# New durations in a planner's list, sums of queries and keys on two engines, and unread products inside the tables

## The chip, the cores and the metric

The kernel runs on one core of one Trainium2 chip. The metric is device microseconds (us) of one launch; one more execution is taken with the hardware profiler, and its trace is what is read here. TensorE (PE) multiplies, with weight loads (PEld) beside it; VectorE (DVE), ScalarE (ACT) and GpSimd (POOL) work elementwise, and SyncE (SP) issues transfers. GpSimd issues the indirect transfers.

## The reference

Two transformer layers on x of 2 x 2048 x 256. Each layer normalises x and adds two things to it: attention and a mixture of experts.

```python
x = L0_attn_x
xn = _layernorm(x, axis=-1)
x = x + _L0_attn_ref(xn, ...) + _L0_ffn_ref(xn, ...)
xn = _layernorm(x, axis=-1)
x = x + _L1_attn_ref(xn, ...) + _L1_ffn_ref(xn, ...)
```

Layer 0 attends causally with 16 heads of 16 over 2048 rows, keys and values shared by groups of four heads; queries and keys come through low-rank matrices and are turned by rotary tables (`x1 * cos - x2 * sin`, `x1 * sin + x2 * cos`). Its experts: each row goes to the best two of eight, with places up to a capacity of 1280 each, `gelu(a) * g`, and a gated sum. Layer 1 attends to 32 fixed patterns with sparsemax, and has eight experts and a shared one. The change touches layer 0 alone.

## The kernel before

**The stages.** Layer 0's attention, and six of its eight experts woven into it, are one hand-made stream (to about 1400 us in the trace); then experts 6 and 7 run; then layer 1, which another planner (class Plan) orders. Layer 1 is not changed.

**What the stream holds.** The attention takes 32 units j (a batch, a block of 512 queries, and a group of heads). For each j: *maxima* (line 530, tile s): TensorE multiplies queries with keys in 64-row halves, VectorE takes each row's maximum from PSUM (line 550); the maxima of a whole j are flipped (mtT) and placed by a transfer into the queries as further rows, so that the scores come out with the maximum subtracted. *Scores* (line 579, tile sc): 128 x 512 products, and ScalarE's exponential (line 589) frees the PSUM bank; there are two such banks. On the diagonal GpSimd masks the result (line 591, affine_select). *Values* (line 594, tile av): four groups of 32 columns side by side. Then VectorE transposes, GpSimd scales (line 616), and the output projection follows (po).

**Preparation.** Groups of 512 rows are fetched, normalised, flipped (tp), and brought to low rank (lw). Cosine and sine *tables* of a block of 512 positions (line 406, tile cs) are spread from 16 partitions to 128: two products with 16 rows, then a copy by ScalarE. A *rotary step* (lines 452 to 475) makes queries or keys: TensorE products (pab), VectorE multiplies with the tables (line 460), GpSimd adds the two halves (line 1016, "the sum"), ScalarE rounds the result (line 467, "the conversion"), GpSimd subtracts to get the remainder (line 474, "the difference"), and SyncE writes both to DRAM, from where the queries and keys are loaded. There are 24 such steps, 8 for keys and 16 for queries.

**Routing and scatters.** When all groups' logits are there, VectorE ranks the experts and computes each row's slot. Then GpSimd scatters 32 tiles of rows to the experts' buffer: for each tile SyncE loads the row (line 729), GpSimd writes a tag (line 733) and issues two indirect transfers (line 736). When all are sent, the woven experts begin: turning (ext), hidden products (exh), down products (exy), scaling, and an indirect accumulation into x1 (line 811).

**What sets the order.** Every instruction is pinned in the order in which the list loop (line 1501) emits it. The loop keeps a modelled clock for each engine (`T`) and picks, among the candidates for TensorE, the one with the least price: its wait, a switch of layout (SWX), and weights such as EXB, IDLE, FILL, RUN. Work of the other engines is emitted by `later` and `flush` (lines 850 and 854) when its inputs are ready in the model. `scatter` (line 1190) emits a tag or a transfer when GpSimd's modelled clock has passed. `add_group` and the due times GRP0 and GRPN say when preparation should come; MOST bounds the lead of maxima, TAIL says how early the woven experts should be done. A score is the unit in which places in the list are given here: "score 192" is after 192 of the 1280 score products.

**Unread products.** Where the model expects TensorE to wait before the woven experts begin, `fill` (line 1476) emits bfloat16 products whose result nobody reads (tile idle), one per 150 modelled ns of wait, unless a share of recent activity is reached; `keep_up` (line 1492) adds them where that share is short. `STREAM` (line 822) says how much each kind of work counts as activity.

Of the kernel before, what the change touches and what calls it, by code (L numbers as in the profile page):

```python
# [11 lines left out]
F32 = mybir.dt.float32  # L12
I32 = mybir.dt.int32
F32R = mybir.dt.float32r
BF16 = mybir.dt.bfloat16
AF = mybir.ActivationFunctionType
ALU = mybir.AluOpType
# [6 lines left out]
P = 128  # L24
# [8 lines left out]
ROW = E + 2  # L33
# [116 lines left out]
def moe_transformer_kernel(  # L150
# [8 lines left out]
    V, A, G, PE, SP = nc.vector, nc.scalar, nc.gpsimd, nc.tensor, nc.sync  # L159
# [23 lines left out]
    ones = keep.tile([P, P], F32, name="ones")  # L183
# [109 lines left out]
    with ExitStack() as actx:  # L293
# [38 lines left out]
        def pin(ins):  # L332
            return tc.keep_in_program_order(ins)

        def mm(*args, **kw):
            pin(PE.matmul(*args, **kw))  # L336
# [62 lines left out]
        def load_tables(blk):  # L399
# [3 lines left out]
            for i, ap in enumerate((cos, sin)):  # L403
                sdma(cs16[blk][0:16, i], ap[0:16, 512 * blk:512 * blk + 512])

        def tables(blk):

            ps = ps2.tile([P, 2, 512], F32, tag="ps2", name="cs128")
            for i in range(2):
                mm(ps[:, i], lhsT=sel16.rearrange("k a b -> k (a b)"), rhs=cs16[blk][0:16, i], start=True, stop=True)  # L410
            pin(A.copy(cs_sb[:, :, 512 * blk:512 * blk + 512], ps))

        def fetch(grp):
# [53 lines left out]
            pin(A.copy(hi, tt[:, 0]))  # L467
            return hi

        def rope_low(tt, r, hi):  # L470
            n = tt.shape[0]
            at = 2048 + 512 * r
            lo = scr[:n, at:at + 512].bitcast(F32R)
            pin(G.tensor_tensor(lo, tt[:, 0], hi.bitcast(F32), ALU.subtract))
            return lo

        kss, qs, vas = {}, {}, {}
# [154 lines left out]
        def add_sum(bq):  # L632
            pin(G.dma_start(x1[0:NT].rearrange("(t p) d -> p t d", p=P)[:, 4 * bq:4 * bq + 4], xos[bq], accum_op=ALU.add))
# [185 lines left out]
        nch = lambda j: 4 * (j // 4 % 4) + 4  # L819
        INF = 10 ** 9  # L820
        HOP, SWITCH, ISSUE, LAND, BYTE = 150, 200, 620, 2300, 0.003
        STREAM = {"v": 0.34, "r64": 0.72, "r128": 0.72, "c": 0.12, "g": 0.2, "f": 0.8, "s": 0.85}
        FULL = dict.fromkeys(("t", "l", "p", "f", "o", "r64", "r128", "v"), "sc")
        T = dict.fromkeys(("PE", "V", "A", "G", "S", "D"), 0)
        model = {"mode": "", "scores": 0.0, "maxima": 0.0, "n": 0}
# [4 lines left out]
        def on(eng, dur, ready=0):  # L830
            T[eng] = max(T[eng], ready) + dur
            return T[eng] + HOP
# [10 lines left out]
        def shift(n, ready):  # L843
            T["D"] = max(T["D"], ready) + n * BYTE
            return T["D"] + LAND - 500
# [4 lines left out]
        def later(eng, dur, ready, f, then=None, rank=1):  # L850
            jobs.append([rank, len(jobs) + model["n"], eng, dur, ready, f, then])
            model["n"] += 1

        def flush():
            now, done = T["PE"], False
            for job in sorted(jobs, key=lambda z: z[:2]):
                rank, _, eng, dur, ready, f, then = job
                if ready > now or (eng == "S" and T["S"] > now + ISSUE):
                    continue
                if eng in ("VL", "AVL"):  # L860
                    held = T["G"]
                    if eng == "VL":
                        eng = "V"
                        if held > now + 300 and now < ready + 3000:
                            continue
                    else:
                        eng = "A" if T["A"] + 70 <= max(T["V"], held) else "V"
                        if T[eng] > now + 300:
                            continue
                        dur, g = dur[eng == "V"], f  # L870
                        f = lambda: g(eng)
                    if eng == "V":
                        ready = max(ready, held)
                elif eng == "AV":
                    eng = "A" if T["A"] <= T["V"] else "V"
                    if T[eng] > now + 300:
                        continue
                    dur, g = dur[eng == "V"], f
                    f = lambda: g(eng)
                elif eng == "V" and T["V"] > now + 300 and now < ready + 5000:  # L880
                    continue
                if eng in "AG" and rank > 1 and T[eng] > now:
                    continue
                jobs.remove(job)
                moved[0] = 0
                f()
                end = on(eng, dur, ready)
                if eng == "S":
                    end = max(end + LAND, shift(moved[0], end))
                if then:  # L890
                    then(end)
                done = True
            return done
# [12 lines left out]
        def give(r, i, t):  # L906
            r[i] = t
# [4 lines left out]
        def use2(dur_pe, mode, ready, f):  # L912

            f()
            return pe(mode, dur_pe, max(ready, free2[-2]))
# [77 lines left out]
            at["lg", grp] = free2[-1]  # L993

        def p_tables(b):
            t = use2(1720, "c", 0, lambda: tables(b))
            free2.append(on("A", 1000, t))
            at["cs", b] = free2[-1]
            give(xt, cs16["ring", b], t)

        def rope(n, products, done):
            box = {}
            key = ("tt", ropes["n"] % 2)
            t = use2(1720, "r%d" % n, 0, lambda: box.update(zip(("tt", "r"), products())))
            free2.append(on("V", 1220, t))
            at[key] = INF

            def summed(t):
                def high(t):
                    def low_(t):  # L1010
                        at[key] = t
                        done(box, 1, t)
                    done(box, 0, t)
                    later("G", 1270, t, lambda: box.update(lo=rope_low(box["tt"], box["r"], box["hi"])), low_, 0)
                later("A", 610, t, lambda: box.update(hi=rope_high(box["tt"], box["r"])), high, 0)
            later("G", 1270, free2[-1], lambda: pin(G.tensor_tensor(box["tt"][:, 0], box["tt"][:, 0], box["tt"][:, 1], ALU.add)),
                  summed, 0)

        def both(key, f):
# [87 lines left out]
        for s, j in enumerate(order):  # L1107
            b, qb = j // 16, j // 4 % 4
            first_use.setdefault(("k", b, qb), s)
            first_use.setdefault(("q", j // 2), s)  # L1110
        LEAD, MOST, EXB, SWX, RUN, ALONE, JOIN, IDLE, GAIN, GRP0, GRPN, QK0, QKN, FILL, TAIL = 2.5, 20.0, 243.0, 215.8, 2, 62.2, 125.5, 72.4, 5092.0, 15.0, 5.5, 36.4, 2.7, 136.0, 11.8
        tab, made = set(), set()
        natural = []

# [55 lines left out]
        def p_project(bq, i0):  # L1170
            if i0 == 0:
                at["xoi", bq] = take(xg)
            t = use2(1720, "p", 0, lambda: project(bq, i0))
            free2.append(on("V", 700, t))
            if i0 == 2:
                at["atts"] -= 1
                adds.append((free2[-1], 1100, lambda: add_sum(bq), lambda t: give(xg, at["xoi", bq], t)))

        def accumulate():
            now = T["PE"]  # L1180
# [9 lines left out]
        def scatter():  # L1190
            if "routed" not in at or at["routed"] > T["PE"] or scat["ti"] == NTILE:
                return
            now = T["PE"]
            while scat["loaded"] < min(NTILE, scat["ti"] + 3) and row_free[-3] is not None and row_free[-3] <= now:
                ti = scat["loaded"]
                if when("kept", ti // 4) > now:
                    break
                scat["loaded"] += 1
                take(row_free)
                later("S", ISSUE, now, lambda ti=ti: load_row(ti), lambda t, ti=ti: at.update({("row", ti): t}), 2)  # L1200
            if T["G"] > now:
                return
            ti = scat["ti"]
            if scat["tagged"] < ti:
                if when("row", ti) <= now:
                    scat["tagged"] = ti
                    tag_row(ti)
                    on("G", 190)
            else:
                dispatch(ti, scat["k"])  # L1210
                end = max(on("G", 1250) + 3500, shift(4 * P * ROW, T["G"]) + 1200)
                scat["k"] += 1
                if scat["k"] == 2:
                    give(row_free, 3 + ti, end)
                    scat["k"], scat["ti"] = 0, ti + 1
                    at["sent"] = end
# [239 lines left out]
        for i in range(NSLOT // 512):  # L1456
            later("S", ISSUE, 70000 + 7000 * i, lambda i=i: clear(buf, i), None, 2)
            later("S", ISSUE, 470000 + 40000 * i, lambda i=i: clear(buf1, i), None, 2)
        idle = ones.bitcast(BF16)

        def product():

            if "idle" not in exs:
                exs["idle"] = psex.tile([P, 512], F32, tag="ex", name="idle")
            rows, cols = (64 if model["mode"] == "s" else P), (32 if model["mode"] == "av" else P)
            mm(exs["idle"][0:cols, 0:256], lhsT=idle[0:rows, 0:cols], rhs=idle[0:rows], start=True, stop=True)

        COUNT, SHARE, EACH, LEAST = 3413, 0.65, 150, 0.56
        gap = {"sum": 0, "n": 0}

# [1125 lines left out]
```

## Time and profile before

| what | value |
|---|---|
| median of 3 runs | 1925.57 us (1925.03 to 1931.07) |
| the profiled execution's own time | 1926.28 us |
| its span, first to last instruction | 1924.5 us |
| mean granted TensorE clock | 0.983 |
| PE busy | 1848.5 us, 96% |
| DVE, ACT, POOL busy | 1225.9, 1016.6, 647.3 us |
| unread products (idle) | 469, busy 75.8 us |
| scatters (line 736) | 64 from 264 to 416 us |
| first turning of the woven experts (ext) | 427.4 us |

A windows view gives for each stretch the busy time of each engine and the granted clock (1.00 is full). A timeline gives instructions in order of time: start, length, engine, line, operation, tiles, count, and in brackets how long the engine was idle before it and what ended that. Matmuls overlap, so a busy TensorE is not one at its peak; a full group of 512 score columns takes it about 0.28 us with its start, though its row says 0.5. Lines of the kernel's helper functions stand for all their callers: line 336 is `mm`, 339 `flip`, 345 `sdma`; they are told apart by the tile.

### The profile page before, as it was taken

Reading aid. Unit: us, or ns where it says so; the run is one execution under the profiler, and the core shown is the slowest. Engines: PE = TensorE matmul, PEld = TensorE weight load, DVE = VectorE, ACT = ScalarE, POOL = GpSimd, SP = SyncE. Lnnn points to the kernel's source line nnn. Section 1 sums busy time; section 2 is a strip of 40 time slices with the busy share of each in tenths; the row PEclk is TensorE's granted clock in tenths of the full one; section 3 lists DMA queues with packets and bytes.
Section 4 is the critical chain, followed back from the end, with each engine's and each line's share of the span. In section 5 each row is a group of like instructions: output and inputs, shape, how many; then the busy total and the mean of one; then the engine's idle time right before and its main releaser. Section 6 shows DMA issues by size and latency. Waiting matters only on the chain.

```text
span 1924.5 us, 29201 instructions
## 1 busy us (share of the span) xinstructions
PE 1848.5 (96%) x10597; PEld 1123.2 (58%) x10597; DVE 1225.9 (64%) x2754; ACT 1016.6 (53%) x1901; POOL 647.3 (34%) x856
## 2 busy tenths in 40 slices
PE   9999899999999999999999999999899899999996
PEld 5545454445655656665665566566466456577864
DVE  5776776677676664667666765664122659985555
ACT  5355443556667667556676666677511442344351
POOL 6232367631222213212222211222222117756550
PEclk9999999999999999999999999999899899999999
DMA  4565556430223314333222221210242302354526
GB/s 136 161 182 152 166 149 198 158 103 13 64 52 89 94 40 130 88 83 83 76 56 65 67 64 32 55 43 10 39 109 27 113 12 91 136 165 156 184 104 264
DMA packets 131851, 192.89 MB, mean 100 GB/s; under 512 B 17261, under 2 KB 105843, under 8 KB 131570
## 3 DMA queue, kind: packets, MB, share of 16 engines
q1 hardware_dynamic: 103378, 137.18, 23.0%
q0 software_dynamic: 27072, 53.08, 11.7%
q8 instruction: 87, 1.43, 0.3%
q10 hardware_dynamic: 1248, 0.67, 0.1%
q14 instruction: 66, 0.54, 0.1%
HBM read 102.44 MB, written 95.77 MB: 103 GB/s over the span
## 4 chain that ended last, share of the span: by engine, by line
PE 76%; issue 6%; DVE 6%; POOL 5%; ACT 4%; DMA 3%; POOLq 0%; SPq 0%; ACTq 0%; DVEq 0%
PE sc L336 16%; PE av L336 12%; PE s L336 11%; PE exh L336 10%; PE exy L336 5%; PE gu L142 4%; PE po L142 3%; DVE part L550 3%; PE acc L142 2%; PE pz L142 2%; PE pab L336 2%; PE idle L336 1%; PE po L336 1%; ACT es L589 1%; POOL xn L142 1%
## 5 line engine op out<-in xcount | busy, mean ns | idle before, releaser
L589 ACT ACTIVATE es<-sc 128x512 f32<-128x512 f32 (+3 forms) x1280 | 636.3, 531 | 467.3 <-PE sc L336 443.3
L550 DVE TENSOR_REDUCE part<-s 128x2 f32<-128x1024 f32 (+3 forms) x640 | 650.2, 1059 | 217.4 <-PE s L336 216.5
L336 PE MATMUL sc<-q,ks 128*128 128x512 f32 (+3 forms) x1280 | 534.0, 466 | 13.6 <-ACT es L589 11.4
L336 PEld LDWEIGHTS sc<-q,ks 128*128 128x128 f32 x1280 | 221.3, 190 | 172.6 <-ACT es L589 87.0
L336 PE MATMUL av<-es,va 128*32 128x512 f32 (+3 forms) x2560 | 278.8, 541 | 3.3 <-POOL es L591 2.4
L591 POOL TENSOR_SCALAR_AFFINE_SELECT es<-es 128x256 f32<-128x256 f32 x256 | 108.2, 424 | 486.3 <-ACT es L589 485.6
L336 PE MATMUL s<-ks,q 64*128 64x512 f32 (+3 forms) x1280 | 231.5, 428 | 9.3 <-DVE part L550 5.9
L336 PEld LDWEIGHTS s<-ks,q 64*128 64x128 f32 x1280 | 102.8, 186 | 173.0 <-DVE part L550 77.5
L336 PEld LDWEIGHTS av<-es,va 128*32 128x32 f32 x2560 | 65.4, 109 | 119.8 <-issue 100.8
L811 POOL DMA_INDIRECT x<-low,tox x54 | 85.4, 1581 | 114.6 <-issue 49.5
L336 PE MATMUL exh<-cs_sb,low 128*128 128x256 f32 (+1 forms) x480 | 121.6, 360 | 0.0
L336 PE MATMUL exh<-cs_sb 128*128 128x256 f32 (+1 forms) x480 | 120.9, 360 | 0.0
L779 DVE COPY agx<-exh 128x512 f32<-128x512 f32 (+1 forms) x89 | 56.3, 632 | 87.6 <-PE exh L336 81.7
L142 POOL DMA_INDIRECT buf<-xn,slot x64 | 72.6, 1134 | 94.5 <-DVE rc L142 75.3
L787 POOL TENSOR_TENSOR agx<-agx 128x1024 f32<-128x1024 f32 (+1 forms) x18 | 37.1, 2058 | 193.3 <-ACT agx L783 172.6
L142 POOL DMA_INDIRECT oe<-xn,to x72 | 81.6, 1134 | 58.8 <-ACT xn L142 41.7
L336 PEld LDWEIGHTS exh<-cs_sb 128*128 128x128 f32 x480 | 84.9, 189 | 14.0 <-issue 1.1
L336 PEld LDWEIGHTS exh<-cs_sb,low 128*128 128x128 f32 x480 | 84.9, 189 | 12.6 <-issue 0.4
L142 DVE MAX8 srt<-z 128x8 f32<-128x16 f32 x1024 | 81.0, 158 | 9.9 <-ACT z L142 9.9
L336 PE MATMUL idle<-ones 128*128 128x256 bf16 (+2 forms) x469 | 75.8, 293 | 1.2 <-POOL ones L184 1.2
L736 POOL DMA_INDIRECT buf<-xsr,idx_sb x64 | 63.5, 993 | 28.2 <-issue 8.6
L142 PE MATMUL gu<-xg,xn 128*128 128x256 f32 x288 | 65.7, 380 | 0.8 <-DMA xn<-wall,which 0.8
(330 smaller groups left out, 2454.5 us busy)
## 6 DMA issues: line engine op xcount, KB each, us to landing
q<-qd SPq DMA_DIRECT2D x128, 128.0 KB
buf<-zero SPq DMA_DIRECT2D x20, 516.0 KB
buf<-zero SPq DMA_DIRECT2D x20, 514.0 KB
xn<-buf SPq DMA_DIRECT2D x18, 514.0 KB
qd<-agx SPq DMA_DIRECT2D x32, 256.0 KB
xsr<-xnd SPq DMA_DIRECT2D x32, 256.0 KB
oe<-zero SPq DMA_DIRECT2D x16, 512.0 KB
xn<-oe SPq DMA_DIRECT2D x16, 512.0 KB
```

Source lines behind the costliest of these rows:

```text
L142: return lambda *a, **k: self.tc.keep_in_program_order(f(*a, **k))
L336: pin(PE.matmul(*args, **kw))
L550: pin(V.tensor_reduce(parts[j][:, i, 2 * pair:2 * pair + 2, kb], sc[:, :, :n], AX.X, ALU.max))
L589: pin(A.activation(es[:, g % 2, :n], sc[:, :n], AF.Exp, scale=0.25))
L591: pin(G.affine_select(es[:, :, 0:P], es[:, :, 0:P], pattern=[[0, 2], [1, P]], compare_op=ALU.is_ge, fill=0.0, base=0, channel_multiplier=-1))
L736: pin(G.indirect_dma_start(ways[(2 * ti + k) % 8], bass.IndirectOffsetOnAxis(ap=idx_sb[:, k, ti:ti + 1], axis=0), xsr[:, ti % 3, k], None, ...
L779: pin((A.copy if eng == "A" else V.tensor_copy)(ag[i % 2][:, :, f, 0:n], exs["ps"][:, :, 0:n]))
L787: pin(eng.tensor_tensor(a, a, g, ALU.mult))
L811: pin(G.indirect_dma_start(x1[:], bass.IndirectOffsetOnAxis(ap=exs["to", i][:, c:c + 1], axis=0), ysx[:, c], None, compute_op=ALU.add))
```

## The change

Five things, all in layer 0's stream:

- Durations in the model: a tag on GpSimd 190 to 260 ns, a scatter 1250 to 1290, a sum or difference 1270 to 1300, an accumulation of the projected rows 1100 to 1450, the tables 1720 to 2360.
- A sum or difference is a job "GV": if GpSimd would end later than VectorE would by more than ROPEV (17 ns), and VectorE is free within 300 ns, VectorE does it, at a modelled 680 ns.
- Between and after the two products of a table stand three unread products each; the tables' share of activity goes from 0.12 to 0.36.
- Retuned weights: MOST 20.0 to 18.1, EXB 243.0 to 247.4, SWX 215.8 to 195.8, IDLE 72.4 to 104.2, GRP0 15.0 to 14.5, GRPN 5.5 to 4.1, FILL 136.0 to 149.8, TAIL 11.8 to 13.3.
- `product` moves ahead of `tables`, which now calls it.

```diff
         def tables(blk):
             ps = ps2.tile([P, 2, 512], F32, tag="ps2", name="cs128")
             for i in range(2):
                 mm(ps[:, i], lhsT=sel16.rearrange("k a b -> k (a b)"), rhs=cs16[blk][0:16, i], start=True, stop=True)
+                for _ in range(3):
+                    product()
...
-        def rope_low(tt, r, hi):
+        def rope_low(tt, r, hi, eng):
...
-            pin(G.tensor_tensor(lo, tt[:, 0], hi.bitcast(F32), ALU.subtract))
+            pin(eng.tensor_tensor(lo, tt[:, 0], hi.bitcast(F32), ALU.subtract))
...
-        STREAM = {"v": 0.34, "r64": 0.72, "r128": 0.72, "c": 0.12, "g": 0.2, "f": 0.8, "s": 0.85}
+        STREAM = {"v": 0.34, "r64": 0.72, "r128": 0.72, "c": 0.36, "g": 0.2, "f": 0.8, "s": 0.85}
...
+                if eng == "GV":
+                    late = max(T["G"], ready) + dur[0] > max(T["V"], ready) + dur[1] + ROPEV and T["V"] <= now + 300
+                    eng, dur, g = "V" if late else "G", dur[late], f
+                    f = lambda: g(V if late else G)
...
-            t = use2(1720, "c", 0, lambda: tables(b))
+            t = use2(2360, "c", 0, lambda: tables(b))
...
-                    later("G", 1270, t, lambda: box.update(lo=rope_low(box["tt"], box["r"], box["hi"])), low_, 0)
+                    later("GV", (1300, 680), t, lambda eng: box.update(lo=rope_low(box["tt"], box["r"], box["hi"], eng)), low_, 0)
...
-            later("G", 1270, free2[-1], lambda: pin(G.tensor_tensor(box["tt"][:, 0], box["tt"][:, 0], box["tt"][:, 1], ALU.add)),
+            later("GV", (1300, 680), free2[-1], lambda eng: pin(eng.tensor_tensor(box["tt"][:, 0], box["tt"][:, 0], box["tt"][:, 1], ALU.add)),
...
-                adds.append((free2[-1], 1100, lambda: add_sum(bq), lambda t: give(xg, at["xoi", bq], t)))
+                adds.append((free2[-1], 1450, lambda: add_sum(bq), lambda t: give(xg, at["xoi", bq], t)))
...
-                    on("G", 190)
+                    on("G", 260)
...
-                end = max(on("G", 1250) + 3500, shift(4 * P * ROW, T["G"]) + 1200)
+                end = max(on("G", 1290) + 3500, shift(4 * P * ROW, T["G"]) + 1200)
```

Since the list is computed from these numbers, the order of the whole stream of layer 0 changes, on every engine.

More of the change, by code (lines that the diff above doesn't have):

```diff
@@ L404, in load_tables, with product @@
                 sdma(cs16[blk][0:16, i], ap[0:16, 512 * blk:512 * blk + 512])
+        idle = ones.bitcast(BF16)
+        def product():
+            if "idle" not in exs:
+                exs["idle"] = psex.tile([P, 512], F32, tag="ex", name="idle")
+            rows, cols = (64 if model.get("mode") == "s" else P), (32 if model.get("mode") == "av" else P)
+            mm(exs["idle"][0:cols, 0:256], lhsT=idle[0:rows, 0:cols], rhs=idle[0:rows], start=True, stop=True)
         def tables(blk):
@@ L859, in flush @@
                     continue
-                if eng in ("VL", "AVL"):
+                if eng == "GV":
+                    late = max(T["G"], ready) + dur[0] > max(T["V"], ready) + dur[1] + ROPEV and T["V"] <= now + 300
+                    eng, dur, g = "V" if late else "G", dur[late], f
+                    f = lambda: g(V if late else G)
+                elif eng in ("VL", "AVL"):
                     held = T["G"]
@@ L1110, in moe_transformer_kernel @@
             first_use.setdefault(("q", j // 2), s)
-        LEAD, MOST, EXB, SWX, RUN, ALONE, JOIN, IDLE, GAIN, GRP0, GRPN, QK0, QKN, FILL, TAIL = 2.5, 20.0, 243.0, 215.8, 2, 62.2, 125.5, 72.4, 5092.0, 15.0, 5.5, 36.4, 2.7, 136.0, 11.8
+        LEAD, MOST, EXB, SWX, RUN, ALONE, JOIN, IDLE, GAIN, GRP0, GRPN, QK0, QKN, FILL, TAIL, ROPEV = 2.5, 18.1, 247.4, 195.8, 2, 62.2, 125.5, 104.2, 5092.0, 14.5, 4.1, 36.4, 2.7, 149.8, 13.3, 17.0
         tab, made = set(), set()
@@ L1458, in moe_transformer_kernel @@
             later("S", ISSUE, 470000 + 40000 * i, lambda i=i: clear(buf1, i), None, 2)
[L1459 to L1466, printed above, removed]
         COUNT, SHARE, EACH, LEAST = 3413, 0.65, 150, 0.56
```

## The prediction

> **What bounds the kernel now.** I read the windows by stage first, then the timeline where TensorE's granted clock falls, then the waits. The columns of a windows row are: stretch, length, busy time (instructions) of PE, PEld, DVE, ACT and POOL, then granted clock, DMA share, GB/s.
>
> ```profile
> 300.00:400.00 100.00, 93.96 (x535) 42.97 (x536) 64.73 (x72) 49.22 (x98) 67.15 (x93) 0.91 0.53 162
> 600.00:700.00 100.00, 99.23 (x644) 60.61 (x642) 67.81 (x82) 66.39 (x119) 22.29 (x29) 1.00 0.26 66
> ...
> 330.00:335.00 5.00, 3.12 (x4) 1.51 (x5) 0.22 (x1) 2.19 (x4) 3.13 (x3) 0.58 0.44 127
> 335.00:340.00 5.00, 5.00 (x17) 3.33 (x15) 1.80 (x3) 1.68 (x3) 2.22 (x3) 0.50 0.16 51
> 340.00:345.00 5.00, 5.00 (x26) 1.84 (x24) 2.56 (x3) 1.59 (x3) 4.11 (x6) 0.56 0.41 149
> ```
>
> From 420 to 1365 us layer 0 is bound by TensorE: 99% busy, clock 1.00. What the list loses lies before 420: there the 469 unread products (busy 75.8 us, 0.16 each) stand for waits that the list expects, and there the clock drops. So time is gained by losing less of TensorE before 420; the work itself stays. Two losses are GpSimd's lateness. The first, from the timeline:
>
> ```profile
> 329.40 1.29 POOL L1016 TENSOR_TENSOR agx<-agx 64x512 f32<-64x512 f32 x1
> ...
> 330.72 0.62 ACT L467 CAST agx<-agx 64x512 fp32r<-64x512 f32 x1 [3.44 <-POOL agx L1016]
> 331.24 1.07 ACT L589 ACTIVATE es<-sc 128x512 f32<-128x512 f32 x2
> 331.88 0.29 PEld L336 LDWEIGHTS sc<-q,ks 128*128 128x128 f32 x1 [3.10 <-ACT es L589]
> 331.88 0.80 PE L336 MATMUL sc<-q,ks 128*128 128x512 f32 x1 [2.82 <-ACT es L589]
> ```
>
> The products for the sum at 329.40 were done at 325.00, but two tags and four scatters stood ahead of it on GpSimd. ScalarE's conversion waited 3.44, the exponentials stood behind it, and TensorE waited 2.82 for a free score bank, then ran at half clock to about 344. The second:
>
> ```profile
> 392.55 0.97 POOL L736 DMA_INDIRECT buf<-xsr,idx_sb  x1 [0.30 <-issue]
> 393.54 0.41 POOL L591 TENSOR_SCALAR_AFFINE_SELECT es<-es 128x256 f32<-128x256 f32 x1
> ...
> 394.00 1.05 PE L336 MATMUL av<-es,va 128*32 128x512 f32 x4 [1.91 <-POOL es L591]
> ```
>
> A causal mask waited behind scatters, and the values behind the mask; the clock was 0.56 and 0.75 in the next two stretches of 5 us. After the tables of blocks 2 and 3 the clock also fell (0.80 and 0.85 at 140 to 150, 0.66 at 200 to 205):
>
> ```profile
> 143.61 3.29 PE L336 MATMUL idle<-ones 128*128 128x256 bf16 x16
> ...
> 201.40 3.41 PE L336 MATMUL idle<-ones 128*128 128x256 bf16 x16
> ```
>
> Sixteen products take 3.3 us there, 0.2 each.
>
> **The change, part by part.** It alters a planner, so I count in the order that both kernels are built with. The sum goes against the profiled execution: 1926.28 us, span 1924.5 and 1.8 around it; the median of the runs, 1925.57, is 0.7 lower.
>
> *Waits the list expects.* The new order holds 448 products for 469; 24 are the tables' own, so 424 are left as filling, 45 fewer. At 0.16 each: -7.3. Of the 24, 12 belong to blocks 0 and 1 in the start-up, where TensorE waits anyway; 12 stand in the stream: +1.9 at 0.16 (1.3 at the 0.107 of full clock). Taken: -5.4. Ends: +1.9, if filling only moves into unfilled waits, and -6.0. This includes a place that gets worse: between scores 192 and 193 products go from 36 to 59.
>
> *The late sum.* In the new order the pair of sums around score 206 still has two tags and four scatters between them, so the second is as late as before. But TensorE has more to do meanwhile. Before: two scores (0.28 each), eight value matmuls (0.99), four maxima matmuls with mask (1.0), two scores, eight values, four maxima (0.6), two scores, three products (0.3): 5.6 us. After: one score, eight values, four maxima, two scores, sixteen values (1.85), maxima with mask, two scores, four matmuls of query products (1.72): 7.6. The 2.82 shrinks to 0.8: -2.0. The half clock of 330 to 345 lost 5 x (0.42 + 0.50 + 0.44) = 6.8, about 0.8 of it inside the wait: -6.0 if it does not fall.
>
> *The late mask.* Between the first and second mask of that diagonal the old order has two tags and four scatters, the new one a tag and two scatters. A tag with two scatters takes 2.73 on GpSimd (338.71 to 341.44), so the mask ends at 391.2 for 393.95, and the second half of the values wants it at about 391.5: -1.9, and -3.4 of clock (5 x 0.44 + 5 x 0.25).
>
> These two are worth 0 to -13.3. What is late next is VectorE's maxima (1.219 each, VectorE 65 busy of 100 there) and the landing of rows for the scatters. I take half, -6.7, since regained TensorE time meets those.
>
> *Sums on VectorE.* Only 4 of 48 go there (three sums, one difference). The nearest row without company, a VectorE 128x512 tensor_tensor, takes 0.685; but a 128x256 one of the routing (line 267) took 0.426 alone and 1.282 at 222.0, beside a sum on GpSimd that started at 221.76. So 0.69 to 1.97 each (0.685 plus GpSimd's 1.28); at most 5 us of VectorE if all four meet such company. [...] I take 0.69 for three and cover by other work, because most of GpSimd's queue there is scatters. Behind such a sum stand maxima on VectorE, and TensorE's bank waits for those; the sum around score 232 would else stand behind a tag and scatters. Counted at nothing; uncovered, +5 at most.
>
> *Tables.* The clock lost 5 x (0.20 + 0.15 + 0.34) = 3.4 at two tables. Products between the halves may hold it; but 13 products of filling still follow each table for 16, so the list itself still expects the activity to be short. 0 to -3.4; taken -1.0, near nothing, since no row shows a table with products between.
>
> *Runs.* TensorE changes between score, maxima and value layouts 871 times for 843. Eight value matmuls start 0.99 apart from what follows, 24 take 2.71: 0.13 to 0.14 per run beyond the 0.107 each. 13 of the 28 lie after score 512 in the bound stage: +1.8; 15 before it: 0 to 2.1, taken 1.0.
>
> *The end of layer 0.* After the last expert matmul 23 scores are left for 18; ScalarE sets the pace there (0.55 each at 1379 to 1390). 0 to +2.8, taken +1.0.
>
> *Other terms.* SyncE's queue has 643 instructions in both; its order moves (tables and row loads later, first query load earlier), no transfer is added. The durations for x1 accumulations, retuned weights and group due times act through the order counted above. Layer 1 is untouched.
>
> Sum: -5.4 - 6.7 - 1.0 + 2.8 + 1.0 = -9.3: **1917.0 us**.
>
> On the clock, the row shows half rate from about 332 to 344 while TensorE was busy nearly throughout. [...]
>
> **Rivals.** (1) *The wait at score 192 becomes the bound; slower.* Before the flip of the next tile's maxima, the new order holds four units of maxima there where the old has two: four more reductions of 1.219, +4.9. The list hides this behind products; but if VectorE is later than it expects (routing, line 267's 1.28), the following scores start late and the bunched rotary work (products from score 168 on, earlier before) runs into the scatters. Then the half-clock stretches return elsewhere and the two gains are nil: +1.9 for the table products without the filling gain, +3.9 runs, +1.0 end, +4.9: +11.7, 1938. It decides once the regained waits are under some 6 us. For it: VectorE is 70 to 76 busy of 100 from 100 to 300 us. Against: the order holds fewer products in six of the nine stretches of 32 scores from 32 to 320.
> (2) *Gains move, nothing is left.* GpSimd's stalls go, but as many stalls come from ScalarE waiting for VectorE, as at 199.04 (1.70) and 214.62 (1.77) now, each with 1.6 of clock: two new ones +6.7: 1923.7.
> (3) *The change does not do what it says*: VectorE's sums are held by GpSimd and the masks still wait; +5 on the forecast without the halved 6.7's mask part (2.7): 1924.7.
>
> **Numbers.** Forecast 0.54; rival 1 0.23; rivals 2 and 3 together 0.23. About 0.3%, 5.8 us, is what a measurement of this kernel can tell from no change: the forecast is faster by more, rivals 2 and 3 lie within, rival 1 is slower. Faster 0.54, same 0.23, slower 0.23. With all ends at their best, -6.0 - 13.3 - 3.4, it is 1903.6; worst is rival 1 near 1938, with the end at +2.8 1940. I leave out the outermost of both: 1905 to 1935.
>
> **What would show it.** Right: no TensorE wait over 1 us for exponentials behind a conversion, none for masks during scatters, clock 0.97 or more in 300 to 400, fewer products' time (about 65 us), first expert turning earlier than now (427.4). Wrong: clock digits that fall elsewhere before 420, a VectorE sum of 1.3 us or more, a wait at score 193 longer than now.

## The result, and the profile after

The changed kernel is slower: 1935.37 us (median of 20 runs) for 1927.64 of before on the same chip, ratio 1.0038, 95% interval 1.0027 to 1.0048. The forecast was 1917.0; the time lies 0.4 us above the range of 1905 to 1935, on the side of rival 1. The profiled execution has a span of 1934.1.

The windows by stage, the same columns as before, first one line of the kernel before:

```profile
200.00:300.00 100.00, 93.47 (x565) 49.14 (x563) 76.41 (x107) 40.47 (x87) 55.35 (x67) 0.97 0.58 170
```

The changed kernel:

```profile
200.00:300.00 100.00, 92.41 (x511) 47.02 (x507) 73.95 (x104) 38.63 (x80) 48.28 (x58) 0.91 0.55 158
300.00:400.00 100.00, 93.28 (x518) 43.59 (x514) 67.67 (x74) 49.69 (x96) 66.41 (x89) 0.93 0.61 179
...
600.00:700.00 100.00, 96.81 (x617) 57.58 (x619) 67.11 (x80) 62.05 (x112) 22.52 (x28) 0.98 0.23 57
```

The clock is a little better from 300 to 400 (0.93 for 0.91), worse from 200 to 300 (0.91 for 0.97), and something new is lost in the bound stage: 96.81 of 100 busy and clock 0.98 from 600 to 700, where before had 99.23 and 1.00. In windows of 5 us:

```profile
185.00:190.00 5.00, 5.00 (x27) 1.99 (x24) 2.88 (x3) 1.64 (x4) 0.82 (x2) 1.00 0.90 258
190.00:195.00 5.00, 5.00 (x24) 2.87 (x24) 0.90 (x1) 1.78 (x3) 0.41 (x1) 1.00 0.02 5
...
225.00:230.00 5.00, 5.00 (x23) 2.44 (x22) 3.95 (x15) 1.67 (x3) 0.41 (x1) 1.00 0.14 45
230.00:235.00 5.00, 5.00 (x46) 2.67 (x44) 3.83 (x7) 1.98 (x6) 1.44 (x2) 1.00 0.10 31
...
280.00:285.00 5.00, 5.00 (x17) 2.84 (x16) 2.16 (x2) 0.00 (x0) 4.69 (x5) 0.50 0.95 268
285.00:290.00 5.00, 5.00 (x9) 2.05 (x9) 1.22 (x2) 0.00 (x0) 1.67 (x2) 0.54 0.85 153
...
300.00:305.00 5.00, 5.00 (x18) 3.30 (x15) 2.36 (x2) 0.00 (x0) 2.91 (x5) 0.50 0.71 225
...
330.00:335.00 5.00, 2.62 (x3) 1.18 (x4) 2.82 (x3) 1.31 (x3) 3.48 (x4) 0.55 0.66 178
335.00:340.00 5.00, 5.00 (x23) 3.06 (x25) 2.82 (x4) 2.13 (x4) 1.28 (x1) 0.76 0.11 37
```

In this trace the fall after the late mask (395 to 405) is gone. The tables of blocks 2 and 3 have moved: their products start at 187.8 and 226.3 us, for 141.4 and 199.4 before, and the clock is 1.00 around them. The fall after the late sum is still there (330 to 340), and two new ones stand at 280 to 290 and around 300. **The late sum**, from the timeline:

```profile
328.40 1.29 POOL L1031 TENSOR_TENSOR agx<-agx 64x512 f32<-64x512 f32 x1
...
329.72 0.62 ACT L478 CAST agx<-agx 64x512 fp32r<-64x512 f32 x1 [3.84 <-POOL agx L1031]
...
330.37 1.09 DVE L485 TENSOR_TENSOR agx<-agx 64x512 fp32r<-64x512 f32 x1 [3.87 <-ACT agx L478]
...
331.39 1.81 DVE L561 TENSOR_REDUCE part<-s 128x2 f32<-128x768 f32 x2
...
332.38 3.78 PE L336 MATMUL pab<-low,wq 96*128 96x512 f32 x4 [4.09 <-DVE part L561]
```

The sum is late behind four scatters, as before. But now its difference (line 485) is one of the four that went to VectorE. VectorE stands in front of it for 3.87 us until ScalarE has converted the sum; two maxima reductions are queued behind; TensorE's next product, of queries (pab), needs their bank and waits 4.09, where TensorE waited 2.82 before. **The break at score 192:**

```profile
279.53 3.42 PE L336 MATMUL idle<-ones 64*128 64x256 bf16 x15
282.88 3.78 PE L336 MATMUL pab<-low,wkv 96*128 96x512 f32 x4
286.45 3.43 PE L336 MATMUL pab<-low,wq 96*128 96x512 f32 x4
...
291.19 0.73 PE L336 MATMUL s<-ks,q 64*128 64x512 f32 x4
...
297.57 1.02 PE L339 MATMUL mtT<-ident,mt 128*8 128x128 f32 x4 [0.60 <-DVE part L561]
...
305.04 0.99 PE L336 MATMUL sc<-q,ks 128*128 128x512 f32 x1
```

From one exponential to the next it is 30.5 us here, from 275.6 on; before it was 13.6, from 288.2. Two rotary steps stand between the maxima, at half clock (3.78 and 3.43 for 1.88), and VectorE is idle meanwhile (4.60 us ahead of line 471 at 286.77).

**In the bound stage** the trace shows what TensorE waited for between 430 and 700 us (engine, line, releaser: us in total, times, longest). Before:

```profile
PE mtT L339 <- DVE mt L562: 0.9, 2, 0.5
PE sc L336 <- ACT es L589: 0.7, 2, 0.4
PE s L336 <- ACT mr L427: 0.2, 1, 0.2
```

After:

```profile
PE sc L336 <- ACT es L600: 2.5, 4, 0.9
PE mtT L339 <- DVE part L561: 1.8, 1, 1.8
PE s L336 <- DVE part L561: 0.7, 2, 0.4
PE mtT L339 <- DVE mt L573: 0.7, 3, 0.3
PE s L336 <- ACT mr L438: 0.4, 2, 0.2
```

1.8 us of waits have become 6.1. The longest is worth a look:

```profile
636.40 2.35 POOL L798 TENSOR_TENSOR agx<-agx 128x1024 f32<-128x1024 f32 x1
...
636.66 2.12 DVE L568 CAST mh<-nm 128x16 fp32r<-128x16 f32 x1
...
639.61 0.60 PE L339 MATMUL mtT<-ident,mt 128*8 128x128 f32 x4 [1.80 <-DVE part L561]
...
641.12 3.21 PE L336 MATMUL av<-es,va 128*32 128x512 f32 x16
```

A cast of 128x16 took 2.12 on VectorE, beside a product of GpSimd that started 0.26 earlier; its median in the 32 casts is 0.175. The flip waited 1.80 for it, and then the clock fell (0.66 from 640 to 645; sixteen values took 3.21 for the usual 1.9).

### The profile page after: what moved, and what is told of

It is laid out like the page before. It is cut to its first block, busy times and chain, and to the rows that moved or that the text cites. A ratio compares the mean times of both kernels' runs of the same rounds, so it can differ in the third digit from the quotient of the medians.

```text
span 1934.1 us, 29156 instructions
## 1 busy us (share of the span) xinstructions
PE 1849.2 (96%) x10564; PEld 1122.1 (58%) x10576; DVE 1223.3 (63%) x2750; ACT 1017.8 (53%) x1906; POOL 648.6 (34%) x855
## 4 chain that ended last, share of the span: by engine, by line
PE 51%; issue 5%; DVE 4%; ACT 3%; POOL 2%; DMA 2%; POOLq 0%; ACTq 0%; SPq 0%; DVEq 0%
PE sc L336 10%; PE av L336 8%; PE exh L336 7%; PE s L336 6%; PE exy L336 4%; PE po L142 3%; PE gu L142 3%; PE acc L142 2%; PE pz L142 1%; DVE srt L142 1%; DVE part L561 1%; PE pa L1632 1%; PE pg L1632 1%; POOL oe L142 1%; PE po L336 1%
## 5 line engine op out<-in xcount | busy, mean ns | idle before, releaser
L336 PE MATMUL sc<-q,ks 128*128 128x512 f32 (+3 forms) x1280 | 526.3, 461 | 13.5 <-ACT es L600 11.5
L798 POOL TENSOR_TENSOR agx<-agx 128x1024 f32<-128x1024 f32 (+1 forms) x21 | 43.0, 2050 | 185.6 <-ACT agx L794 185.6
```

Of the source, the lines that this page charges most:

```text
L798: pin(eng.tensor_tensor(a, a, g, ALU.mult))
```

## The experiments

All ratios are against the kernel before, timed beside it on the same chip. The chips of these runs take some 55 to 70 us more than the first one, most of it behind layer 0's last values (578 to 589 us, for 533), before and after alike; so only ratios are compared, and, between kernels timed together, means of 12 runs. "First turning" is the first flip of a woven expert (ext), "woven" the time from there to layer 0's last values. Three traces of the changed kernel have their first turning at 435.8, 446.2 and 435.9: where the clock falls before 430 differs from execution to execution, so a profile alone can't weigh a few us there. The woven stage repeats within 1.6 us.

| kernel | ratio, 95% interval | first turning | woven |
|---|---|---|---|
| before (first chip; again) | 1 | 427.4; 440.3 | 963.8; 962.2 |
| after (first chip; again; third) | 1.0038 (1.0027 to 1.0048); 1.0036 (1.0009 to 1.0063); 1.0037 (1.0015 to 1.0060) | 435.8; 446.2; 435.9 | 965.8; 966.5; 967.1 |
| only_gv | 0.9988 (0.9969 to 1.0006) | 442.4 | 959.3 |
| only_tables | 1.0022 (0.9997 to 1.0047) | 442.0 | 959.6 |
| only_weights | 1.0008 (0.9989 to 1.0026) | 437.7 | 968.1 |
| only_durs, twice | 0.9978 (0.9955 to 1.0001); 0.9969 (0.9944 to 0.9995) | 450.9; 452.3 | 949.6; 949.4 |
| after_allg | 1.0019 (0.9994 to 1.0044) | 435.1 | 966.3 |
| after_noprod | 0.9999 (0.9969 to 1.0028) | 434.5 | 966.1 |
| after_noprod01 | 1.0029 (1.0007 to 1.0051) | 439.2 | 966.3 |
| after_noprod23 | 1.0007 (0.9980 to 1.0034) | 442.6 | 966.1 |
| after_bare | 0.9989 (0.9970 to 1.0009) | 432.9 | 966.3 |
| before_prod | 1.0012 (0.9989 to 1.0036) | 439.6 | 962.3 |
| bare_oldwoven | 0.9998 (0.9973 to 1.0022) | 433.3 | 969.7 |
| before_newwoven | 1.0064 (1.0039 to 1.0090) | 445.6 | 971.8 |
| ctrl_hop | 0.9922 (0.9894 to 0.9950) | 425.8 | 961.9 |
| ctrl_dur | 1.0024 (0.9995 to 1.0053) | 437.5 | 968.2 |

The woven stage begins after 317 scores in before, after 322 in the changed order, after 332 in only_durs; a later beginning leaves less to do in it.

**One part each, on the kernel before.** The theories: A, the move to VectorE costs; B, the retuned weights cost; C, every new number draws a new order, and that decides.

```diff
 only_gv:      + the "GV" branch, line 474's engine as an argument, later("GV", (1270, 680), ...)
 only_tables:  + three product() after each half, "c": 0.36, use2(2360, ...)
 only_weights: + MOST 18.1, EXB 247.4, SWX 195.8, IDLE 104.2, GRP0 14.5, GRPN 4.1, FILL 149.8, TAIL 13.3
 only_durs:    + on("G", 260), on("G", 1290), later("G", 1300, ...) twice, adds ... 1450
```

> The kernel before with one part of the change alone: sums and differences may go to VectorE (GpSimd's modelled duration stays 1270). Theory A (the move itself costs: a difference given to VectorE waits there for ScalarE's conversion, with maxima queued behind it, and TensorE waited 4.09 us for those at 332 in the changed kernel): slower by 4 to 8 us, 1.002 to 1.004, with a TensorE wait of 3 us or more for line 550's maxima while VectorE is idle ahead of a difference. Theory B (the retuned weights place the preparation and the routing badly, so the break at score 192 and the woven stage cost): within 2 us of before. Theory C (each new number draws a new order of the whole list, and the one of before is a good draw): slower by 3 to 10 us, with losses at places that have nothing to do with the moved sums.

> The kernel before with one part alone: three unread products after each half of a table, 2360 for 1720 in the model, and the share 0.36. Theory A and theory B: -2 to +2 us, the table products cost 1.9 and the clock's falls at 140 to 150 and 200 to 205 are gone. Theory C: slower by 3 to 10 us, by a break or clock fall before 420 that before does not have, and by other layout changes in the woven stage.

> The kernel before with the eight retuned weights alone (no sum on VectorE, no table products, old durations). Theory B: slower by 7 to 12 us, 1.004 to 1.006, with a break of 20 us or more around score 192 and 8 us lost between scores 512 and 704. Theory A: within 3 us of before. Theory C: anywhere between -2 and +10 us, the losses not at the places of the changed kernel.

> The kernel before with the durations alone: tag 260, scatter 1290, sum and difference 1300 (all on GpSimd), accumulation 1450. Theories A and B: -3 to +2 us, the order hardly matters for 3 per cent more on GpSimd. Theory C: slower by 3 to 10 us, as for the other parts.

No part alone is measured as slow as the whole, though the interval of only_tables reaches it. A's forecast for only_gv fails in the time (0.9988), but not for want of the waits. Six differences and four sums run on VectorE there, and one difference meets a late sum:

```profile
341.08 0.62 ACT L467 CAST agx<-agx 128x512 fp32r<-128x512 f32 x1 [6.48 <-POOL agx L1020]
...
341.73 0.69 DVE L474 TENSOR_TENSOR agx<-agx 128x512 fp32r<-128x512 f32 x1 [6.54 <-ACT agx L467]
...
342.02 0.80 PE L336 MATMUL s<-ks,q 64*128 64x512 f32 x2 [5.55 <-ACT va L427]
```

VectorE stands idle for 6.54 us in front of it, and TensorE for 5.55: by the trace not for maxima (its longest wait for those from 240 to 430 is 0.6) but for a copy on ScalarE (va) that stood behind the same late conversion. One long wait does not decide the time of a whole order. B fails for only_weights (+0.08%), although its break at score 192 is 21.5 us long. C's "slower by 3 to 10" holds at most for only_tables; the durations alone are, if anything, a gain. Whether the parts add up can't be read from these runs, since each of them redraws the list.

**The additions taken back, the order kept.** To part the order from what is issued, the list of the changed kernel was kept and only the issue edited:

```diff
 after_allg:      -    f = lambda: g(V if late else G)
                  +    f = lambda: g(G)
 after_noprod:    -    for _ in range(3): product()          (in tables)
 after_noprod01:  +    for _ in range(3 if blk >= 2 else 0): product()
 after_noprod23:  +    for _ in range(3 if blk < 2 else 0): product()
 after_bare:      after_allg and after_noprod together
 before_prod:     kernel before, +  for _ in range(3): product()   (model unchanged)
```

> The changed kernel as it is, beside the parts. If the whole is more than its parts (each part alone was within 0.25 per cent of before), it is again 1.003 to 1.005 of before, and layer 0 ends 7 to 10 us later than in the kernel before taken on the same chip. If the difference belongs to one chip, the ratio is within 0.2 per cent of 1.

> The kernel before, one look for its trace on this chip. Layer 0 ends 7 to 10 us earlier than in the changed kernel's trace of the same chip if the loss is the change's own, and within 3 us if it is the chip's.

The loss is the change's own, not the chip's: 1.0036. The last values come at 1412.7 for 1402.5, though the profiled execution was the slowest of its twelve (1998.86 us for a median of 1991.61).

> The changed kernel's list, order and engines, but the three sums and the one difference that go to VectorE are issued on GpSimd at the same places; nothing else moves. Theory A (the moved difference at 330 keeps VectorE idle for 3.87 us until ScalarE's conversion, with maxima behind it, and TensorE waits 4.09 us): that wait goes to 1 us or less and the clock's fall at 330 to 340 with it, 4 to 6 us less than the changed kernel. Rival (the sum ahead of it is late behind four scatters on GpSimd, which a move of the difference does not touch, and ScalarE's exponentials are behind the conversion): a TensorE wait of 2.5 us or more stays, for exponentials in place of maxima, and the time is within 2 us of the changed kernel.

2.7 us less than the changed kernel timed beside it (means; plus or minus 2.6). At the place itself theory A is plain. The timeline of after_allg:

```profile
324.25 1.29 POOL L1031 TENSOR_TENSOR agx<-agx 64x512 f32<-64x512 f32 x1
...
325.20 1.98 PE L336 MATMUL pab<-low,wq 96*128 96x512 f32 x4 [1.05 <-DVE part L561]
...
325.57 0.62 ACT L478 CAST agx<-agx 64x512 fp32r<-64x512 f32 x1 [3.84 <-POOL agx L1031]
...
326.84 1.28 POOL L485 TENSOR_TENSOR agx<-agx 64x512 fp32r<-64x512 f32 x1
```

The sum and the conversion are exactly as late (3.84), but TensorE waits 1.05 for 4.09, and the clock stays 1.00 from 320 to 345. The rival's long wait for exponentials came as well, at a later sum. In the changed kernel that sum is one of the three on VectorE and relieves ScalarE:

```profile
357.93 0.68 DVE L1031 TENSOR_TENSOR agx<-agx 64x512 f32<-64x512 f32 x1
...
358.65 0.62 ACT L478 CAST agx<-agx 64x512 fp32r<-64x512 f32 x1 [0.56 <-DVE agx L1031]
```

In after_allg it is late behind GpSimd's scatters:

```profile
352.57 1.27 POOL L1031 TENSOR_TENSOR agx<-agx 64x512 f32<-64x512 f32 x1
...
353.88 0.62 ACT L478 CAST agx<-agx 64x512 fp32r<-64x512 f32 x1 [4.83 <-POOL agx L1031]
...
354.83 0.74 PE L336 MATMUL sc<-q,ks 128*128 128x128 f32 x2 [2.96 <-ACT es L600]
```

TensorE waits 2.96 there, and the clock is 0.54 from 355 to 360. So the moves bring one wait and take another away. The 2.7 is what is left of both; it is less than the 4 to 6 expected, and its interval comes close to nothing.

> The changed kernel's list, but the 24 products inside the tables are not issued (the model still counts them); the order of everything else is the same. If they hold the clock: it falls to 0.8 or less for 5 us at two or three tables before 220, and the time is 1 to 4 us more than the changed kernel. If they are only cost: no such fall, 1 to 2 us less than the changed kernel.

6.3 us less than the changed kernel (plus or minus 3.4): more than "only cost" allowed. Without the products the clock is 1.00 from 140 to 230, over both tables (184.7 and 222.1 us); so it is not they that hold it in this order. Where the 6.3 lies can be estimated from the span and the granted clock that every run lists: the share of the clock not granted, times the span, comes to 49.6 us in the changed kernel's twelve runs and to 44.6 without the products. That is 4.9 of the 6.3 (plus or minus 3.9), and the 1.4 left over is about the products' own time.

> The changed kernel without the 12 products of the first two tables, the start-up's; the 12 of blocks 2 and 3 stay. Theory S (the start-up is a chain on TensorE, and the 12 lengthen it: 1.3 us up to the first flips, 1.0 more up to the rotary products at 37 to 39): the first exponential comes 2 to 5 us earlier, the time is 2 to 6 us below the changed kernel. Theory M (those of blocks 2 and 3 cost, in the bound stream): within 1.5 us of the changed kernel. The prediction had the start-up's 12 at nothing and the others at 1.9.

> The changed kernel once more, beside the others of this call as their reference: 1.003 to 1.005 of before.

Theory S falls: 0.4 us more than the changed kernel timed beside it (plus or minus 3.3), and the first exponential comes at 58.8 for 58.7. The start-up's twelve cost nothing that can be measured.

> The changed kernel without the 12 products in the tables of blocks 2 and 3; those of the first two tables stay. If these 12 are the cost: 4 to 7 us below the changed kernel (0.9995 to 1.0015 of before), of which 2.0 are their own time of 0.16 each and the rest comes later, where the stream meets the scatters. If neither half alone costs (the run that left out all 24 was a lucky one): 1.003 to 1.004 of before.

1.0007 (0.9980 to 1.0034), where the changed kernel had 1.0036 to 1.0038 in other comparisons. This points to the twelve of blocks 2 and 3, with about 6 us by the ratios, but the intervals overlap and the changed kernel was not timed beside it, so the share of each half is not shown. Their own time is 1.3 to 1.9 (twelve at 0.11 to 0.16).

> The kernel before with the 24 table products issued and nothing else changed: its list does not know of them, the order is the same. Theory S: 4 to 7 us slower than before (1.002 to 1.0035), the first exponential 2 to 5 us later. The prediction's step (12 at nothing, 12 at 0.16, clock falls at the tables of 140 to 150 and 200 to 205 gone): -2 to +2 us.

1.0012: nothing that is certain. Its first exponential is at 68.8 for 68.7, against theory S; and the clock still falls to 0.91 at 140 to 160 and 0.83 at 200 to 220, against the hope that products between the halves hold it.

> The changed kernel's list and order, with both additions taken back where they are issued: the 24 table products are left out and the four moved sums and differences are on GpSimd. What is left is the new order alone. If the two costs add (6.3 and 2.7 us, as the two runs alone measured them), it is 9 us below the changed kernel and 0.998 to 1.000 of before: the order is worth -4 to 0 us. Rival (the two runs measured the same thing, a stream that comes later into the scatters): 5 to 6 us below the changed kernel, 1.000 to 1.002. If the order is what costs (the break at score 192, the woven stage): 1.002 or more.

8.6 us below the changed kernel timed beside it (plus or minus 3.0), as if the two costs, 2.7 and 6.3, add. **The new order alone stands at 0.9989 of before (0.9970 to 1.0009), some -2 us and not told from nothing,** where the prediction's terms for it come to -10.2 (its -9.3 with the tables' +1.9 and -1.0 taken out).

**Where a gain of the order could go.** The break between exponentials at score 192 is 23.6 us in after_bare too (22.9 to 30.5 in the nine traces of this order), for 13.6 to 14.3 in the five of the old one; it is not all lost, since rotary steps run in it. Still, the first turning of after_bare is 7 us earlier than in before_again and before_prod (432.9 for 440.3 and 439.6), with five more scores done. This is no proof of a gain. By the traces' clock records TensorE runs at half clock for 23.8 us before the first turning in after_bare and for 34.0 in before_again, which is 5 of the 7 us, and the three traces of the changed kernel alone lie between 20.4 and 47.6. Then the woven stage takes 966.3 for 962.2 with five scores fewer. Theory W: the retuned weights cost there.

```diff
+            if scat["ti"] == NTILE:
+                MOST, EXB, SWX, IDLE, TAIL = ...   (old values on after_bare; new ones on the kernel before)
```

> The new order without the additions (no table products issued, sums on GpSimd), and from the last scatter on the old values of MOST, EXB, SWX, IDLE and TAIL; up to there the order is the same. Theory W (the retuned weights cost in the woven stage, seen as waits of 6.1 for 1.8 us between 430 and 700 and a clock fall at 640): from the first turning to the last values 959 to 961 us for 966.3, waits 430 to 1000 below 5 us, and 0.995 to 0.997 of before. Rival (the stage is entered with another lead of maxima and scores, whatever the weights): 965 to 967 us, waits as before, 0.998 to 1.000.

> The kernel before, and from the last scatter on the new values of MOST, EXB, SWX, IDLE and TAIL; up to there it is the kernel before. Theory W: 968 to 970 us from the first turning to the last values, for 962.2 to 963.8, and 1.002 to 1.004 of before. Rival: 962 to 965 us and within 0.15 per cent of before.

The two halves disagree. New weights on the old order: 971.8 for 962.2, and 1.0064. Old weights on the new order: 969.7 for 966.3, no gain at all. So the weights by themselves are not what costs; the waits suggest that each pair of weights and entering state draws its own stalls. TensorE's waits from 700 to 1000 us in before_newwoven begin with

```profile
PE mtT L339 <- DVE mt L562: 2.3, 3, 1.7
PE s L336 <- DVE part L550: 2.2, 4, 0.7
```

where the kernel before has 1.8 in all. The 1.7 is once more a cast (2.00, at 994.04) beside GpSimd's product. Of ten traces, before, before_again and ctrl_hop have no such meeting that slows the cast (their longest cast is 0.53); the changed kernel, after_bare, only_gv, only_durs and before_newwoven have one of 2.0 to 2.1, bare_oldwoven and ctrl_dur two.

**Controls: a change without meaning.**

```diff
 ctrl_hop:  -HOP, SWITCH, ... = 150, 200,        +HOP, SWITCH, ... = 152, 200,
 ctrl_dur:  -on("G", 1250) + 3500                +on("G", 1255) + 3500
```

> The kernel before with the durations alone, once more: it was 0.9978 [0.9955, 1.0001]. If that part is a gain, 0.997 to 0.999 again; if it was chance, 0.999 to 1.001.

> The kernel before with one meaningless change in the model: the hop between engines 152 for 150 ns. The order changes on every engine from the start-up on (453 unread products for 469). Redraw theory: off by 3 us or more to either side (below 0.9985 or above 1.0015), with the stage from the first turning to the last values 3 us or more from 962.3. Rival (the order of the list moves the time only where a changed number has a cause): within 0.1 per cent of before, and that stage at 961 to 964.

> The kernel before with a scatter at 1255 for 1250 ns in the model; the order is that of before up to about score 256, other after it (1778 layout changes by the count that gives 1812 for before). Redraw theory: as for the other control, 3 us or more from before, the first turning as in before and the loss or gain after it. Rival: within 0.1 per cent.

Two nanoseconds in the model's hop make the kernel 0.8% faster, more than any part of the change moved it and better than both kernels. Five in the scatter's duration give 1.0024, which is not told from 1 (0.9995 to 1.0053), but its woven stage is 6.0 us longer, from the same score 317; with the ungranted clock taken out as above, it is 9.5 us slower than before (plus or minus 2.5), and ctrl_hop 7.5 faster (plus or minus 3.2). In the timeline of ctrl_dur:

```profile
984.67 2.34 POOL L787 TENSOR_TENSOR agx<-agx 128x1024 f32<-128x1024 f32 x1 [17.27 <-ACT agx L783]
...
985.03 2.00 DVE L557 CAST mh<-nm 128x16 fp32r<-128x16 f32 x1
...
987.47 0.60 PE L339 MATMUL mtT<-ident,mt 128*8 128x128 f32 x4 [1.75 <-DVE mt L562]
```

ctrl_hop has its first turning at 425.8, 14.5 before that of before_again (another chip) after the same 317 scores, with the clock at 1.00 from 100 to 240 us, where before_again falls to 0.83, 0.90 and 0.93 in three stretches of 20. So a redraw alone moves this kernel by as much as any part of the change, which is theory C, and even the gain of only_durs (0.9978, 0.9969) can't be put down to truer durations.

## Why the prediction was wrong

One step failed in its mechanism (the late sum), one term was mis-sized (the tables), and one assumption hid new waits (that the work stays as it is after 420). The sum that joined them could not carry a change of order.

- **The late sum** (-2.0 and -6.0, halved with the mask) failed in its mechanism. It counted what TensorE has to do meanwhile (7.6 us for 5.6), but looked for the moved instructions on VectorE only where they run, not where they wait. The last piece of that cover, the query products (1.72), is the very one that waits for the bank. That "behind such a sum stand maxima on VectorE" was said in *Sums on VectorE* and priced at nothing. The trace shows 4.09 for the forecast 0.8 and the clock at 0.55: the price at this place is VectorE's wait (3.87), not the length of the instruction (1.09). Taken together the four moves cost 2.7 us (plus or minus 2.6), for 0 taken and 5 at most, while another of them saves a wait of 2.96.
- **Tables** was mis-sized: +1.9 for the twelve in the stream and -1.0 of clock; measured 6.3 (plus or minus 3.4) for all 24, with nothing measurable for the start-up's twelve, as forecast. The two tables no longer stand where the clock fell, and it does not fall there without the products either. By the estimate above most of the 6.3 is clock not granted, against the hope; why twelve products would cost that is not settled.
- **Runs and the end of layer 0** (+1.8 after score 512 and +1.0) missed a loss in the bound stage. I took "the work itself stays" for granted after 420. The woven stage of the new order is 2 to 5 us longer with five scores fewer: waits of 6.1 for 1.8 up to 700, 3.8 for 1.1 to 1.9 up to 1000, and a fall of the clock at 640.
- **The clock terms** (-6.0 and -3.4, halved, and -1.0) did not come about as a whole: estimated as above, the changed kernel loses 2.0 and 0.1 us more to the clock than before in its two later comparisons (plus or minus 3.4), and it is 5.2 and 5.6 us slower without that (plus or minus 1.9).
- **Waits the list expects** (-5.4) and **the late mask** (-1.9 and -3.4) came about in part: products busy 72.0 for 75.8 us. The prediction's "about 65" does not fit its own count, since 448 products at 0.16 are 72. In the first trace one mask wait of 1.62 stands for 1.91, and the clock is 1.00 from 340 to 420; in the other two traces of the changed kernel it falls again, at 395 and at 386. With the additions taken back the first turning is 7 us earlier and five scores further in one trace, which is not enough to call the gain before 420 shown.
- **Rival 1** named the sign and nearly the time (1938). Its mechanism is in the trace: the break at score 192 is 10 to 17 us longer (4.9 was its price), rotary products stand in it and half clock returns (0.50 from 280 to 285). But by itself it does not decide the sign: after_bare keeps this order and a break of 23.6, only_tables has one of 29.7, and neither is clearly slower than before. That its time fits is luck in part. Rivals 2 and 3 did not decide: the stalls that appear are not those of rival 2, and the masks of rival 3 no longer wait behind scatters for long. All three of the prediction's signs of being wrong appear: falls at new places before 420, a sum of 1.41 on VectorE (at 27.16), and the longer break.
- **The form of the sum.** It added parts as if each had its own price. A control without meaning moved the time by -0.8 per cent, so a sum over counted differences of two orders is not good to 0.5 per cent here unless it walks the stalls one by one. (Its best end, 1903.6, also leaves out the +1.8 that has no range; with it, it is 1905.4.)

On the clock: in stretches of 20 us before 430 us the granted clock is mostly 1.00, 0.91 or 0.83 in these traces, steps of 1.7 us lost. A single step (0.66 from 200 to 205 before) is only the shortest fall that they show: the half clock lasted 13.7 us from 330.8 before and 10.2 from 279.3 in the changed kernel.

## What to carry to other kernels

An instruction moved to a less busy engine brings its wait along: ask what it waits for, and what is queued behind it there, before its duration; ask too which wait it takes away. Where a planner pins every order, keep the list and edit only what is issued to price an addition, and change a number that means nothing to learn how far a redraw alone moves the time; a part whose effect is not larger has not been shown to have one. Gains ahead of a bound stage count for little until the bound stage has been read for new waits.

## What the runs showed of the hardware

A VectorE cast of 128x16 takes 0.17 us alone. It took 2.00 to 2.12 where it started 0.26 to 0.38 us into GpSimd's tensor_tensor of 128x1024 (2.34 to 2.35 us), and ended 0.02 to 0.04 after that one (the changed kernel at 636.66, before_newwoven at 994.04, ctrl_dur at 985.03). One that started 2.24 in, near the end (before, at 1318.57), still took 0.17. The cast sits in the chain that turns the maxima, so each such meeting costs TensorE 1.5 to 1.8 us, and in the changed kernel a fall of the clock as well (0.66 from 640 to 645). Why the cast takes so long there is not shown by these runs.

A kernel's granted clock falls at different places in different executions before 430 us (three traces of the changed kernel: 0.92, 0.92 and 0.95 from 240 to 430, with first turnings 10 us apart), while the stage after it repeats within 1.6 us. And the chips differ: from layer 0's last values on it took 578 to 589 us on those of the experiments for 533 on the first, with VectorE idle for 52.3 and 54.5 us ahead of its 1024 MAX8 instructions (before_again and ctrl_hop) for 9.9 in the first chip's trace of before; no run here settles why.
